# When the second image's attention values are emitted, and one pacing constant

## Chip, cores, metric

The kernel runs on one core of a Trainium2 chip. The metric is the device time of one execution in microseconds (us). The core has TensorE (PE; its weight loads are shown as PEld), VectorE (DVE), ScalarE (ACT) and GpSimd (POOL), each with a queue of its own that it executes in order, and SyncE (SP), whose queue issues the transfers (DMA).

## What is computed

The input x is four images of 128 channels and 64 x 64 pixels in float32. Four residual layers follow one another, and each reads the group norm of x (32 groups of four channels, no affine part):

```
x = x + attention(gn(x))      # one head over all 4096 pixels, 128 channels
x = x + conv5x5(gn(x))        # 5 x 5 weights built from two tables and their indices
x = x + scan(gn(x))           # state-space scan, 64 channels forward, 64 backward, 64 states each
x = x + conv3x3(gn(x))        # only main_w and main_b reach the output
```

The scan layer multiplies by Wx, applies a causal convolution of four taps and a silu, makes delta (a softplus), B and C by matrix products, and then runs, for each channel and each of 64 states, h[l] = exp(delta[l] A) h[l-1] + delta[l] x[l] B[l] and y[l] = sum over states of h[l] C[l], plus D x[l]; a last product by Wp gives the layer's output.

## The kernel before

Channels lie on the 128 partitions and the 4096 pixels along the free axis. Each image goes through a *front*: attention, the 5 x 5 convolution, and the *operands* of the scan (delta, delta times x, B and C, written to DRAM in four chunks of 1024 pixels). Then comes its scan, and after that its *back*: the product by Wp and the 3 x 3 convolution.

**Two streams in one program.** The order of instructions is written out by hand, with no reordering by the scheduler, and two Python generators are woven together. `scan_core` emits the scan. `work = images()` emits everything else: the fronts of the images 0 to 3, then the backs. The first image's front runs before any scan; from then on the scan of image b lies beside the front of image b+1, and the backs of images 0 to 2 lie beside the last scan.

**Ticks.** The scan of one image is 256 ticks (4 chunks x 2 directions x 16 groups of states x 2 groups of channels), 1024 for all. In a tick POOL makes the drive `db` (L1588), ACT the decay `da` (L1581, an exponential), DVE runs the recurrence over 1024 pixels (L1598), and the result is multiplied by C. The multiplication is done by DVE (L1601; I call that an *own* tick) or by POOL (L1619; a *pooled* tick). ACT copies the last state (L1614) so that the next chunk can go on from it. Every four ticks PE sums the states into `y` (L1637). Drives run two ticks ahead, the loads of the rows four ticks ahead.

**Narrow and wide form.** PSUM has four banks with the tags s, a, z, y, and four more that are used in one of two ways. In the *narrow* form they hold three half decays of 512 pixels and one bank for the operands, and each tick's decay, recurrence and own multiplication is done in two halves. In the *wide* form they hold two decays of 1024 pixels. `widen` (called once per tick) swaps the form after the recurrence of the tick in which the mark "narrow" is found set or gone.

**Marks.** The generators talk through a set `ready`. `scan_operands(b)` (from L1308 on) is a list of numbered slots, 5 per 512 pixels. It sets "operands" at its beginning, `(b, "taps")` at slot 39, when the last of PE's causal convolutions is out, and "drives" at slot 48. Slots 40 and 50 (first image) or 30 and 50 (the others) hook the logarithms of the softplus, which are emitted in the middle of the next tick (ACT has to load another function table for them and the first one again after them); the generator waits for that with yields of 0.4. After slot 50 it waits for two ticks to begin, emits the last join and drive, takes "operands", "drives" and "narrow" away, and sets `(b, "all")`. With "narrow" gone, the form becomes wide until the next image's convolution has ended and sets it again.

`to_pool(i)` decides which ticks are pooled, by i and by the marks at the time: i % 3 == 2 in the wide form; in the narrow form i % 5 in (0, 2, 4) while "operands" is set, only i % 5 == 1 once "drives" is set, and i % 5 in (1, 3) with neither.

**The values.** `attention_start(b, xn)` of the next image waits until the image before has set `(b - 1, "taps")`, takes the tile V (which held that image's normalised pixels), lets POOL set the column of ones (L483), and emits eight groups of four products of 128 x 128 x 128 on PE (`keys`, L496), each yielding SLOT = 0.7, and each group's copy from PSUM to V on ACT (`take`, L501). A group's bank is s or z in turn, but always s while "operands" is set. `both(...)` runs the operands of image b and the start of image b+1 in turn, one yield of each. When both are at their end, attention begins: a product and ACT's L532, then rounds of scores on PE (L746), exponentials on ACT (L759) and value products on PE (L767), 1.76 per round.

**The pace.** Each yield of `work` carries a cost in planned microseconds of PE. Per tick of scan b the loop hands out PACES[b] of cost, half of it in each half tick:

```
credit = min(credit + pace / 2, pace)
while credit > 0:
    credit -= next(work, pace)
```

Before an image's first tick, `before(b)` runs `work` without scan until `(b, "operands", 0)` is set, if it isn't yet.

Of the kernel before, what the change touches and what calls it, by code (L numbers as in the profile page):

```python
# [44 lines left out]

PRODUCT, VALUES, HOP, SLOT, AHEAD, EARLY = 0.86, 0.9, 1.7, 0.7, 4, 8
LAST_SHARE = 0.75
PACES = 2.60, 2.53, 2.53, 1.53


BQ, BK, BX, BP, CONVB, BD, DSKIP, MAINB, CONVW, ALOG = 0, 1, 2, 3, 4, 5, 6, 7, 8, 12
# [3 lines left out]
def conv_preact_kernel(  # L55
# [37 lines left out]
    pools, ready = {}, set()  # L93
    more = again = None

    def bank(tag, name):
        return pools.get(tag, ps).tile([P, MM], F32, tag=tag, name=name)
# [232 lines left out]
    def stats_tile(name):  # L330
        return small.tile([P, NM, 6], F32, tag=f"gn_st{name[0]}", name=f"st_{name}")
# [75 lines left out]
    def group_norm(st, name):  # L407


        def tile(tag, *shape):  # L410
            return small.tile([P, *shape], F32, tag=f"gn_{tag}", name=f"{tag}_{name}")

        nc.vector.bn_aggr(gcols[:, :, 0], st.rearrange("p a b -> p (a b)"))
        turned, after = gn_work[:, 0], gn_work[:, 1]
        nc.vector.transpose(turned, gcols.rearrange("p a b -> p (a b)"))
        means, vars_ = (
            turned[:, r * 32 : (r + 1) * 32].rearrange("p (g s) -> p g s", s=gsz) for r in range(2)
        )
        var, mean = (
            after[:, r * 32 : (r + 1) * 32].rearrange("p (g s) -> p g s", s=gsz) for r in range(2)  # L420
        )
        total = gn_sums[:, 0]
        nc.vector.tensor_reduce(total, means, AX.X, ALU.add)
        wide = total.unsqueeze(2).to_broadcast([P, 32 // gsz, gsz])
        nc.vector.tensor_scalar(mean, wide, -1.0 / gsz, None, ALU.mult)

        nc.vector.tensor_tensor(means, means, mean, ALU.add)
        nc.vector.tensor_tensor(means, means, means, ALU.mult)
        nc.vector.tensor_tensor(means, means, vars_, ALU.add)
        total = gn_sums[:, 1]  # L430
        nc.vector.tensor_reduce(total, means, AX.X, ALU.add)
        wide = total.unsqueeze(2).to_broadcast([P, 32 // gsz, gsz])
        nc.vector.tensor_scalar(var, wide, 1.0 / gsz, GN_EPS, ALU.mult, ALU.add)
        back = tile("back", 2, 32)
        nc.vector.transpose(back.rearrange("p a b -> p (a b)"), after)
        rs, nb = tile("rs", 1), tile("nb", 1)
        nc.gpsimd.tensor_tensor(rs, back[:, 0, 0:1], mhalf, ALU.pow)
        nc.gpsimd.tensor_tensor(nb, back[:, 1, 0:1], rs, ALU.mult)
        yield HOP
        return rs, nb  # L440

    def normalise(dst, src, gn):
        nc.scalar.activation(dst, src, AF.Identity, scale=gn[0], bias=gn[1])  # L443
# [27 lines left out]
    def attention_start(b, xn):  # L471

        if b == 0:
            st = stats_tile(f"a{b}")
            for i in range(NM):
                nc.vector.bn_stats(st[:, i, :], xn[:, bass.ts(i, MM)])
                yield 0.0
            gn = yield from group_norm(st, f"a{b}")
        while b > 0 and (b - 1, "taps") not in ready:
            yield 0.0  # L480
        v = pools["big"].tile([P, VSIZE], F32, tag="V", name=f"v_{b}")
        v = v[:, : NJT * (C + 1)].rearrange("p (j c) -> p j c", c=C + 1)
        nc.gpsimd.memset(v[:, :, C : C + 1], 1.0)  # L483
        pvs = {}

        def piece(i):
            cut = bass.ts(i, L // 4)
            if b == 0:
                normalise(xn[:, cut], xn[:, cut], gn)

        def keys(i):

            tag = "saz"[i % 3] if b == 0 else "s" if i % 2 == 0 or "operands" in ready else "z"
            pvs[i] = bank(tag, f"pv_{b}_{i}").rearrange("p (t c) -> p t c", c=C)
            for t in range(TPM):
                nc.tensor.matmul(  # L496
                    pvs[i][:, t, :], xn[:, bass.ts(i * TPM + t, P)], wv, start=True, stop=True
                )

        def take(i):  # L500
            nc.scalar.copy(v[:, i * TPM : (i + 1) * TPM, :C], pvs.pop(i))  # L501

        piece(0)
        yield SLOT
        for i in range(NM):
            if i % 2 == 0 and i // 2 + 1 < 4:
                piece(i // 2 + 1)
            keys(i)
            yield SLOT
            if b > 0:  # L510
                take(i)
                yield 0.0
            elif i > 0:
                take(i - 1)
        if b == 0:
            take(NM - 1)
        return xn, v
# [1220 lines left out]
    def program(safe):  # L1738
# [14 lines left out]
        def start(b, after=0):  # L1753

            while b > 0 and (b - 1, "read") not in ready:
                yield 0.0
            for _ in range(after):
                yield 0.0
            xn = large(b, f"x_{b}")[:, :L]
            yield from load(xn, normed[b] if b > 0 else xf[b])  # L1760
            for _ in range(after):
                yield 0.0
            return (yield from attention_start(b, xn))
# [101 lines left out]
        with ExitStack() as es, tc.manual_schedule():  # L1865
# [52 lines left out]
            pools["hc"] = es.enter_context(tc.tile_pool(name=f"hc{safe}", bufs=8))  # L1918
            pace = PACES[0]

            def before(b):
# [3 lines left out]
                while (b, "operands", 0) not in ready:  # L1925
                    next(work)
                pace = PACES[min(b, len(PACES) - 1)]

# [90 lines left out]
```

## Time and profile before

| | us |
|---|---|
| median of 3 runs | 4163.61 (4162.76 to 4168.47) |
| the profiled execution | 4165.07 |
| its span, first to last instruction | 4163.3 |
| mean granted TensorE clock | 0.938 of full speed |

| engine | busy us | share of the span |
|---|---|---|
| PE | 3664.0 | 88% |
| PEld | 2132.6 | 51% |
| DVE | 3509.3 | 84% |
| ACT | 2340.3 | 56% |
| POOL | 3537.9 | 85% |

Milestones in the span, read from the timeline: the first image's operands begin on PE at 625, the first drive of the scan starts at 663.5, the second image's values lie on PE from 679.0 to 712.3 and its scores from 717.4 to 1283. The second image's operands begin on PE at 1468.6, the third's at 2331.7, the fourth's at 3191.3. The last scan instruction ends near 4100, and the last image's back ends the span.

How to read it: a row of the profile's timeline gives the start of an instruction in us from the span's beginning, its length, its engine, its line in the kernel, its operation, the names of the tiles that it writes and reads, and, in square brackets, how long its engine stood idle before it and what ended that. A row of the view by stretches gives, for each engine, the busy time in the stretch and the number of instructions, then the clock that TensorE was granted, the share of time that the DMA engines were busy and what they moved in GB/s. Matmuls in float32 show as two instructions each.

### The profile page before, as it was taken

The page shows a single profiled execution, that of the slowest core. Times are in us where ns is not written, and L with a number is a line of the kernel's source. Part 1 is how long each engine was busy: PE and PEld are TensorE (multiplying, and loading weights), DVE is VectorE, ACT ScalarE, POOL GpSimd, SP SyncE. Part 2 cuts the span into 40 slices and gives each one's busy share as a digit, 9 for nine tenths or more (in the row PEclk, how much of TensorE's full clock was granted, in tenths as well). Part 3 has the DMA queues.
Part 4 walks back from the last instruction along what each step waited for, and adds up shares of the span by engine and source line. Part 5 has one row for each costly group of instructions (what it writes and reads, how often), then busy time and mean ns, then how long its engine had stood idle before and what let it go on. Part 6 is the DMA issues. An engine that isn't in the chain of part 4 may idle for free. (4 is left out here: it accounts for less than half of the span.)

```text
span 4163.3 us, 49791 instructions
## 1 busy us (share of the span) xinstructions
PE 3664.0 (88%) x17626; PEld 2132.6 (51%) x17626; DVE 3509.3 (84%) x2446; ACT 2340.3 (56%) x3925; POOL 3537.9 (85%) x1691
## 2 busy tenths in 40 slices
PE   8999997999999979999999889999899576676746
PEld 4444443888885337777763367777733121221212
DVE  3832216999999989999999889999998899999996
ACT  3344306667675476776654767766645654545442
POOL 3533315999999989999999899999999999999995
PEclk9999998999999989999999999999999788887967
DMA  1021006656555576555555665555656766666661
GB/s 66 30 76 66 3 10 232 211 189 195 191 191 193 194 248 223 199 186 197 191 188 187 232 231 195 193 192 188 203 178 205 273 199 235 206 202 234 208 239 57
DMA packets 224162, 742.39 MB, mean 178 GB/s; under 512 B 29710, under 2 KB 30990, under 8 KB 223644
## 3 DMA queue, kind: packets, MB, share of 16 engines
q1 hardware_dynamic: 223324, 738.73, 52.6%
q8 instruction: 140, 2.29, 0.2%
q14 instruction: 122, 1.00, 0.1%
q10 hardware_dynamic: 576, 0.37, 0.0%
HBM read 663.12 MB, written 75.87 MB: 178 GB/s over the span
## 5 line engine op out<-in xcount | busy, mean ns | idle before, releaser
L1588 POOL TENSOR_TENSOR db<-dx,br 128x1024 f32<-128x1024 f32 x1024 | 2400.0, 2371 | 105.0 <-DVE hc L1598 35.1
L1581 ACT ACTIVATE da<-de,a_neg 128x1024 f32<-128x1024 f32 (+1 forms) x1089 | 1162.1, 1068 | 363.9 <-DVE hc L1601 246.2
L1598 DVE TENSOR_TENSOR_SCAN da<-da,last,db 128x1024 f32<-128x1024 f32 (+1 forms) x501 | 1148.3, 2292 | 24.8 <-ACT da L1581 11.7
L1601 DVE TENSOR_TENSOR hc<-da,cr 128x1024 f32<-128x1024 f32 (+1 forms) x702 | 825.8, 1176 | 60.6 <-DVE da L1598 0.5
L1619 POOL TENSOR_TENSOR hc<-hc,cr 128x1024 f32<-128x1024 f32 x354 | 838.9, 2370 | 19.9 <-ACT last L1614 17.3
L746 PE MATMUL sc<-r,x 128*128 128x256 f32 x3072 | 808.3, 388 | 33.6 <-ACT exchange L759 25.7
L767 PEld LDWEIGHTS acc<-v,exchange 128*128 128x128 f32 x6144 | 801.1, 192 | 47.5 <-issue 10.9
L767 PE MATMUL acc<-v,exchange 128*128 128x129 f32 x6144 | 804.8, 275 | 0.4 <-ACT exchange L759 0.4
L1637 PE MATMUL y<-hc,sel 128*32 128x512 f32 x4096 | 596.8, 649 | 226.8 <-POOL hc L1619 171.6
L746 PEld LDWEIGHTS sc<-r,x 128*128 128x128 f32 x3072 | 530.8, 192 | 203.7 <-ACT last L1614 42.7
L1598 DVE TENSOR_TENSOR_SCAN hc<-da,last,db 128x1024 f32<-128x1024 f32 (+1 forms) x267 | 597.4, 2237 | 12.9 <-ACT last L1614 7.4
L759 ACT ACTIVATE exchange<-sc 128x512 f32<-128x512 f32 x768 | 444.6, 589 | 208.0 <-PE sc L746 195.3
L1637 PEld LDWEIGHTS y<-hc,sel 128*32 128x32 f32 x4096 | 114.1, 113 | 567.9 <-POOL hc L1619 240.2
L1598 DVE TENSOR_TENSOR_SCAN da<-da,db 128x1024 f32<-128x1024 f32 (+1 forms) x169 | 377.3, 2233 | 32.1 <-ACT da L1581 28.3
L568 POOL TENSOR_TENSOR sidep<-sidep,exchange 128x512 f32<-128x512 f32 x120 | 171.1, 1426 | 244.6 <-ACT exchange L550 242.1
L1614 ACT COPY last<-da 128x1 f32<-128x1 f32 x510 | 80.3, 157 | 504.8 <-DVE hc L1601 503.5
L550 ACT ACTIVATE exchange<-sc 128x512 f32<-128x512 f32 x256 | 152.8, 597 | 250.2 <-PE sc L549 246.7
L568 DVE TENSOR_TENSOR sided<-sided,exchange 128x512 f32<-128x512 f32 x120 | 98.1, 817 | 217.5 <-ACT exchange L550 216.2
L556 PE MATMUL acc<-exchange,v 128*128 128x512 f32 x512 | 263.3, 597 | 0.0
L549 PE MATMUL sc<-r,x 128*128 128x512 f32 x512 | 261.9, 594 | 0.8 <-ACT r L532 0.8
L922 PE MATMUL pcm<-xpm,cs 128*128 128x512 f32 x432 | 207.3, 628 | 7.5 <-ACT xpm L443 7.5
L1598 DVE TENSOR_TENSOR_SCAN hc<-da,db 128x1024 f32<-128x1024 f32 (+1 forms) x87 | 190.9, 2194 | 6.6 <-ACT last L1614 3.8
(296 smaller groups left out, 3028.8 us busy)
## 6 DMA issues: line engine op xcount, KB each, us to landing
br<-bm SPq DMA_DIRECT2D x512, 512.0 KB, 4.0
cr<-cm SPq DMA_DIRECT2D x512, 512.0 KB, 4.5
dx<-dxd SPq DMA_DIRECT2D x64, 512.0 KB, 5.3
de<-dd SPq DMA_DIRECT2D x64, 512.0 KB, 6.0
xs<-in_x_dram SPq DMA_DIRECT2D x16, 512.0 KB, 5.6
xsd<-xs SPq DMA_DIRECT2D x16, 512.0 KB, 3.8
bm<-bs SPq DMA_DIRECT2D x32, 256.0 KB, 4.6
xcd<-xc SPq DMA_DIRECT2D x16, 512.0 KB, 3.1
```

Source lines behind the costliest of these rows:

```text
L549: nc.tensor.matmul(sc, xn[:, bass.ts(j, P)], rq[blk], start=True, stop=True)
L556: nc.tensor.matmul(acc[blk], v[:, j, :C], ring[:, u % NRING, :], start=j == 0, stop=j == NJT - 1)
L568: eng.tensor_tensor(s, s, ring[:, u % NRING, :], ALU.add)
L746: nc.tensor.matmul(sc[:, bass.ts(n, HM)], xn[:, bass.ts(2 * k + n, P)], rq[blk][:, cut], start=n == 0, stop=True, skip_group_check=True,)
L759: nc.scalar.activation(pt, sc, AF.Exp)
L767: nc.tensor.matmul(acc[part][:, bass.ts(t, CV)], ring[:, u % NRING, n * HM + t * P : n * HM + (t + 1) * P], v[:, 2 * k + n, :], start=(k, ...
L1581: nc.scalar.activation(da, rep["de", b, c, d, g][:, bass.ts(h, size)], AF.Exp, scale=a_neg[:, at(i)])
L1588: nc.gpsimd.tensor_tensor(dbs[i], rep["dx", b, c, d, g], rows["b", b, c, d, q], ALU.mult)
L1598: nc.vector.tensor_tensor_scan(h, da, db[:, cut], before, ALU.mult, ALU.add)
L1601: nc.vector.tensor_tensor(hc[:, cut], h, rows["c", b, c, d, q][:, cut], ALU.mult)
L1619: nc.gpsimd.tensor_tensor(hcs[i], hcs[i], rows["c", b, c, d, q], ALU.mult)
L1637: nc.tensor.matmul(y[r : r + SG, :], sel, hcs[first + gg][:, bass.ts(h, MM)], start=False, stop=q == NQ - 1, tile_position=(0, r), skip_gr ...
```

## The change

The wait of `attention_start` is for another mark when b is 1, so for the values of the second image alone, and the first constant of PACES is 2.62 instead of 2.60. Nothing else differs; the third and fourth image's values still wait for "taps".

```
-PACES = 2.60, 2.53, 2.53, 1.53
+PACES = 2.62, 2.53, 2.53, 1.53
...
-        while b > 0 and (b - 1, "taps") not in ready:
+        while b > 0 and (b - 1, "all" if b == 1 else "taps") not in ready:
             yield 0.0
```

## The prediction

> **What bounds the kernel now.** I read the page first: the share of busy time of each engine and its 40 slices. The scans fill the span from 650 us on, and there DVE, POOL and, while attention or a convolution lies beside them, PE are all near full. Then I asked for the stretches of the first scan, which is where the change is:
>
> ```profile
> core 0: us, PE busy (x) PEld busy (x) DVE busy (x) ACT busy (x) POOL busy (x), PEclk, DMA share, GB/s
> 665.00:725.00 60.00, 36.54 (x142) 19.69 (x138) 45.21 (x50) 41.53 (x74) 49.94 (x26) 0.85 0.62 226
> 725.00:780.00 55.00, 54.84 (x366) 44.03 (x366) 48.05 (x28) 34.06 (x60) 48.99 (x22) 0.94 0.67 225
> 780.00:1280.00 500.00, 495.18 (x3436) 405.18 (x3429) 486.01 (x279) 352.32 (x638) 490.53 (x212) 1.00 0.59 193
> ```
>
> In 60 us with the operands beside the scan no engine is full; in the 500 us after it three are, within 3%. Ticks show the same: counted by DVE's scans, tick 0 starts at 673.3 and tick 10 at 724.7 (5.13 us each), tick 10 to 20 take 3.67 each, tick 20 to 184 take 3.160. The slow ticks are bound by a chain over in-order queues. DVE, the engine that has to do each tick's scan, waits here (timeline of DVE, columns start, length, operation, idle before it and what ended it):
>
> ```profile
> 690.28 0.70 DVE L1384 SCALAR_TENSOR_TENSOR pb<-u,pb 128x512 f32<-128x512 f32 x1 [4.70 <-ACT u L1413]
> ...
> 715.45 1.23 DVE L1598 TENSOR_TENSOR_SCAN da<-da,db 128x512 f32<-128x512 f32 x1 [2.22 <-ACT da L1581]
> ...
> 719.30 1.22 DVE L1598 TENSOR_TENSOR_SCAN da<-da,db 128x512 f32<-128x512 f32 x1
> ...
> 724.68 2.30 DVE L1598 TENSOR_TENSOR_SCAN da<-da,db 128x1024 f32<-128x1024 f32 x1 [1.43 <-ACT da L1581]
> ...
> 735.87 2.30 DVE L1598 TENSOR_TENSOR_SCAN da<-da,db 128x1024 f32<-128x1024 f32 x1 [4.61 <-ACT da L1581]
> ```
>
> The view of DVE's waits between 675 and 740 sums them: 8.3 for decays, 7.2 for the first image's steps, 0.7, together 16.2 us. Two of them (4.70 and 2.22) follow ACT's logarithms; 1.43 is the swap of the PSUM form; 4.61 is ACT, which stands with an exponential of attention while the next decay is behind it. PE's queue holds the values in between (timeline of PE):
>
> ```profile
> 686.48 2.07 PE L496 MATMUL pv<-wv,x 128*128 128x128 f32 x8 [6.40 <-ACT v L501]
> 688.35 2.86 PE L1364 MATMUL pb<-xc,bdiag 128*128 128x512 f32 x4
> 691.40 1.16 PE L496 MATMUL pv<-wv,x 128*128 128x128 f32 x8 [0.19 <-ACT v L501]
> 696.15 1.13 PE L1364 MATMUL pb<-xc,bdiag 128*128 128x512 f32 x2 [3.59 <-DVE bs L1370]
> ```
>
> With one bank for them (tag s while the operands run) the second group of values stands 6.40 us before a copy on ACT, and the products that the operands need are behind it.
>
> **What the change moves in the plan.** I added up the yields of both generators by hand, half tick by half tick (half the pace each, waits of 0.4 ended by the tick's events). For the old numbers this gives the swap to the wide form after tick 9, as the first 1024-wide scan at 724.68 (tick 10) shows. With the change: up to tick 0.5 nothing differs. Then the operands no longer share their half ticks: the last logarithms are hooked at tick 4 instead of 6, "all" comes at tick 6.0 instead of 8.0, the swap follows tick 7 instead of 9, and the eight groups of values lie in ticks 6.0 to 8.0 instead of 1 to 6.5, now over two banks. Attention begins at tick 8 in both. By 2.62 instead of 2.60 the later stages come one tick earlier: attention ends at 186 instead of 187, the second image's operands begin at 238 instead of 239, and so the third's (493 for 494) and the fourth's (748 for 749). Each narrow stretch there is as long as before. No drain is needed at an image's end: the first chunk of the next is made at tick 248.5 now, 252 is when it is needed.
>
> **The price of each part.**
>
> *Form and pooled ticks, first scan.* From DVE's rows, start to start: an own narrow tick 3.85 (715.45 to 719.30), a pooled narrow one 2.52 (706.84 to 709.36), an own wide one 3.53 (735.87 to 739.40), a pooled wide one 2.20 (742.93 to 745.13). Ticks 4 to 10 are now two pooled and four own narrow and one own wide: 5.04 + 15.40 + 3.53 = 23.97. After: tick 4 turns own (the "drives" mark comes at 3.5), 8 turns pooled, 8 and 9 wide: 11.55 + 2.52 + 2.20 + 7.06 = 23.33. **-0.6 us.** POOL's count of multiplies there is the same.
>
> *DVE's waits, first scan.* Of 16.2 us I keep the two after the logarithms (4.7 + 2.2), the swap 1.4 and the 0.7; the 2.5 for the last piece's u goes, because the product before it no longer stands behind values; for the 4.6 I put 3, since ACT then has eight copies of 0.59 (4.7 us) between the decays of ticks 7 to 9, though PE comes to attention without a gap. 16.2 - 12.0 = **-4.2 us**. Ends: only the logarithms' waits left, -9.3; all kept and the copies added, +4.7.
>
> *The later image ends.* The pooled choice goes by the tick's number, so a shift by one changes it: 258, 513, 762 and 766 are pooled now and own after. Own costs DVE 1.33 more (3.85 - 2.52) and POOL 2.37 less (row L1619 of the page). At 258, 513 and 766, the ticks of a swap, DVE waits 2.40 and 2.15 us for decays (at 1564.62 and 1568.06, the first of the three), which hides it; 762 has no such cover: **+1.3**. Ends: all four, +5.3; POOL was the one waited for at 762, -2.4.
>
> *The pace.* 0.02 more per tick is 158 x 0.02 = 3.2 us in the 500 us where PE is busy 495.2; it still fits, but only just. It shows where PE is full, the 55 us after 725: 17 ticks, **+0.4**. Ends: 0, and 0.02 x 229 ticks of attention and convolution, +4.6. Two other scans speak for the low end: at 2.53 their ticks take 3.157 and 3.163, at 2.60 3.160.
>
> *At nothing:* the memset of v (0.15 on POOL), now behind six more of POOL's steps, nobody before the copies waits for it. The sends of dd and dxd of the last chunk come two ticks earlier in SP's queue; now they hold SP from 708.5 to 720.5 and the row loads behind them, which run four ticks ahead; if that cover were gone, it shows as POOL's 1.5 us wait at 731.34. The new wait for "all" is in the plan alone, no instruction waits for it.
>
> Sum: -0.6 - 4.2 + 1.3 + 0.4 = **-3.1 us**. The profiled execution took 4165.07 (span 4163.3 and 1.8 around it), which gives 4162.0; it was 1.5 above the median of the three timed runs, 4163.61, and it is the median that I forecast: **4160.5 us**.
>
> A rule that speaks against the change. The granted clock in the trace is 0.77 from 680 to 695 and 0.80 from 695 to 710 while values and products share PE, and 0.69 from 725 to 735, when attention starts:
>
> ```profile
> 680.00:695.00 15.00, 5.96 (x21) 0.77 0.33 131
> 695.00:710.00 15.00, 9.69 (x44) 0.80 0.82 277
> 710.00:717.40 7.40, 3.48 (x22) 0.95 0.27 105
> 717.40:725.00 7.60, 4.54 (x12) 0.74 0.35 134
> 725.00:735.00 10.00, 9.84 (x50) 0.69 1.00 350
> ```
>
> The Trainium skill, "TensorE: Matmul & The Clock Gate", Part 1, says that the array runs at half clock by default and at full clock only after a window of about 3.4 us in which it was busy. By that rule, taking the values out leaves PE emptier in ticks 1 to 5, and five products at half clock would each last some 0.9 us more (an estimate from that page), 4.3 us on the operands' chain, with a sum of +1.2 instead of -3.1; the same rule gives some back at attention's start, which then follows the values directly. No row here shows PE without the values, so the sum is left as it is.
>
> **Rivals.**
> *The first scan loses all but the logarithms' waits.* For: the operands' chain is then alone on PE, and copies find two banks. Against: ACT's copies crowd the wide ticks. -0.6 - 9.3 + 0 + 0.4 = -9.5: **4154.1**.
> *POOL holds the first scan, the change does nothing there.* For: from 684.5 to 729.9 POOL has one gap of 0.9; its 44.4 us of steps stay the same ones. Against: by 731 it waits for DVE itself. -0.6 + 0 + 1.3 + 0.4 = +1.1: **4164.7**.
> *TensorE becomes the bound (slower).* The eight groups of values take about 1.05 each (row 679.02), 8.4 us. Now they lie where PE has 23 us idle of 60; then they lie directly before a stretch where it is 54.84 of 55 busy and 99.0% after. If PE never catches up, their 8.4 and the pace's 4.6 show: -0.6 + 8.4 + 4.6 = +12.4, **4176.0**. It decides when exponentials that wait for PE hold up decays by more than DVE's slack in the 500 us (14 us). Against: ticks at 2.53 are no shorter.
>
> **Chances.** Forecast 0.40, first scan frees up 0.22, POOL holds 0.25, TensorE binds 0.13. A measurement of this kernel tells about 0.2% (8.3 us) from no change. Faster by more: the first rival and a little of the forecast, 0.24; slower: the last, 0.13; within: 0.63. The range takes the first two rivals whole and part of the last, with the bounds of the later image ends: 4152 to 4172.
>
> **What would show it.** Swap: the first 1024-wide scan is tick 8, not 10, and two ticks earlier by the clock than 724.68 less what else went. Waits: DVE's sum from tick 1 to 13 near 12 us, no wait of PE for v among products. Image ends: tick 239 to 259 within 2 us of today's 101.4. Pace: ticks 20 to 184 at 3.16; 3.18 or more would be TensorE's rival. The forecast is wrong if DVE's waits at ticks 7 to 10 for decays exceed 8 us, or if an image's end differs by over 4 us, which I have no row for beyond the four moved multiplies.

## The result, and the profile after

The changed kernel takes 4173.27 us (median of 14 runs, 4167.7 to 4178.32), the kernel before 4164.47 beside it (14 runs, 4162.76 to 4168.47): ratio 1.0020, 95% interval 1.0013 to 1.0027. It is **slower by about 8.8 us**, outside the predicted range. The profiled execution of the changed kernel took 4170.89, its span is 4169.1, 5.8 more than before's 4163.3; its runs scatter more (10.6 us against 5.7), so the span shows only part of the median's loss.

Counted by DVE's scans, the time between ticks went as follows (us; the last column is pace_259r of the fourth set):

| ticks | what lies there | before | after | difference | best (old mark, 2.59) |
|---|---|---|---|---|---|
| 0 to 20 | operands, values, start of attention | 88.0 | 85.5 | -2.6 | 84.0 |
| 20 to 184 | attention of the second image | 518.2 | 521.9 | +3.6 | 517.3 |
| 184 to 236 | its convolution | 174.7 | 175.8 | +1.0 | 176.0 |
| 236 to 264 | second image's operands | 131.1 | 127.7 | -3.4 | 129.4 |
| 264 to 490 | attention and convolution, third image | 726.7 | 728.8 | +2.1 | 724.8 |
| 490 to 520 | its operands | 139.5 | 135.6 | -3.9 | 138.1 |
| 520 to 744 | attention and convolution, fourth image | 717.7 | 723.6 | +5.9 | 718.8 |
| 744 to 774 | its operands | 136.2 | 141.6 | +5.4 | 130.6 |
| 774 to 1023 | last scan, backs | 792.5 | 792.2 | -0.3 | 792.1 |

The first scan's stretches, changed kernel (same columns as in the prediction):

```profile
665.00:725.00 60.00, 36.80 (x131) 18.97 (x130) 44.85 (x46) 40.46 (x70) 49.26 (x26) 0.72 0.74 269
725.00:780.00 55.00, 55.00 (x384) 44.00 (x383) 51.02 (x30) 36.05 (x64) 51.87 (x23) 1.00 0.53 182
780.00:1280.00 500.00, 496.27 (x3446) 407.10 (x3445) 483.71 (x277) 352.37 (x639) 488.07 (x211) 1.00 0.58 192
```

PE is now busy in all of the 55 us from 725 (54.84 before) and has 3.7 us left of 500 (4.8 before). DVE and POOL do less in the same 500 us: 483.7 against 486.0, and 488.1 against 490.5. The timeline of DVE, rows with the longest waits:

```profile
687.82 0.69 DVE L1384 SCALAR_TENSOR_TENSOR pb<-u,pb 128x512 f32<-128x512 f32 x1 [3.62 <-ACT u L1413]
...
713.36 2.29 DVE L1598 TENSOR_TENSOR_SCAN hc<-da,db 128x1024 f32<-128x1024 f32 x1 [2.65 <-ACT da L1581]
...
719.65 2.30 DVE L1598 TENSOR_TENSOR_SCAN da<-da,db 128x1024 f32<-128x1024 f32 x1 [4.00 <-ACT da L1581]
...
723.65 2.30 DVE L1598 TENSOR_TENSOR_SCAN da<-da,db 128x1024 f32<-128x1024 f32 x1 [0.39 <-ACT da L1581]
```

The first 1024-wide scan is tick 8, as forecast. The waits of 4.61 and 2.22 are gone; two others, 2.65 and 4.00, stand where ACT now copies the values. The timelines of ACT and, below it, POOL show what these copies wait for:

```profile
704.95 1.32 ACT L1581 ACTIVATE da<-de,a_neg 128x512 f32<-128x512 f32 x2
710.89 1.07 ACT L501 COPY v<-pv 128x512 f32<-128x512 f32 x2 [4.62 <-POOL v L483]
711.85 0.20 ACT L1614 COPY last<-hc 128x1 f32<-128x1 f32 x1
711.95 0.17 ACT L1614 COPY last<-da 128x1 f32<-128x1 f32 x1
712.15 1.12 ACT L1581 ACTIVATE da<-de,a_neg 128x1024 f32<-128x1024 f32 x1
...
718.42 1.12 ACT L1581 ACTIVATE da<-de,a_neg 128x1024 f32<-128x1024 f32 x1
```

```profile
705.86 2.48 POOL L1392 TENSOR_TENSOR exchange<-exchange,u 128x512 f32<-128x512 f32 x2
708.42 2.35 POOL L1397 TENSOR_TENSOR xc<-exchange,xc 128x1024 f32<-128x1024 f32 x1
710.71 0.15 POOL L483 MEMSET v<- 128x32 f32 x1
```

The memset of v stands behind the last joins and the last drive of the operands; ACT's first copy waits 4.62 us for it, and the decay of tick 8 (712.15) is behind that copy. On PE no product of the operands stands behind a value that waits for its bank any more, but the values wait for the copies (7.49):

```profile
684.50 3.78 PE L1364 MATMUL pb<-xc,bdiag 128*128 128x512 f32 x4 [7.29 <-ACT last L1614]
689.89 2.08 PE L1364 MATMUL pb<-xc,bdiag 128*128 128x512 f32 x2 [1.60 <-DVE bs L1370]
...
711.53 8.21 PE L496 MATMUL pv<-wv,x 128*128 128x128 f32 x48 [7.49 <-ACT v L501]
```

A product of 128x512 shows as two instructions. It takes 2.08 us now (689.89) and took 1.13 before, and the stretches show the granted clock beside it:

```profile
680.00:695.00 15.00, 7.93 (x8) 2.18 (x8) 10.87 (x13) 12.98 (x23) 13.62 (x9) 0.50 0.39 158
695.00:710.00 15.00, 6.95 (x32) 3.39 (x32) 13.87 (x15) 8.03 (x13) 14.92 (x8) 0.61 0.74 250
710.00:717.40 7.40, 5.87 (x29) 5.87 (x30) 2.98 (x2) 3.87 (x8) 7.40 (x5) 0.54 0.88 313
717.40:725.00 7.60, 5.96 (x34) 4.51 (x33) 4.87 (x3) 5.69 (x10) 5.07 (x4) 1.00 0.97 348
725.00:735.00 10.00, 10.00 (x73) 7.82 (x72) 8.38 (x6) 6.39 (x12) 8.40 (x4) 1.00 0.46 155
```

The granted clock fell from 0.77 to 0.50 and from 0.80 to 0.61 where the values were taken out, and rose from 0.69 to 1.00 where attention starts.

**The fourth image's end.** SP's timeline, before and then after:

```profile
3268.09 0.51 SPq L1533 DMA_DIRECT2D dx<-dxd  x1
3268.65 1.23 SPq L1561 DMA_DIRECT2D xcr<-xcd  x2
3277.14 0.80 SPq L1393 DMA_DIRECT2D dd<-exchange  x2
3279.62 2.62 SPq L1398 DMA_DIRECT2D dxd<-xc  x2
...
3283.64 0.55 SPq L1533 DMA_DIRECT2D de<-dd  x1
```

```profile
3274.82 0.80 SPq L1393 DMA_DIRECT2D dd<-exchange  x2
3277.31 2.66 SPq L1398 DMA_DIRECT2D dxd<-xc  x2
...
3282.54 0.60 SPq L1533 DMA_DIRECT2D dx<-dxd  x1
...
3285.16 0.55 SPq L1533 DMA_DIRECT2D de<-dd  x1
```

Before, the last sends of dd and dxd are emitted in the first half of tick 765, behind the loads that go out in the second half of tick 764. One tick earlier they are ahead of these loads. SP issues in order here and the sends wait for the join, so the load of dx for tick 769 is issued at 3282.5 instead of 3268.1. POOL's drive for that tick waits for it (POOL after):

```profile
3291.92 4.63 POOL L1588 TENSOR_TENSOR db<-dx,br 128x1024 f32<-128x1024 f32 x2 [7.69 <-DMA dx<-dxd]
```

But it isn't this drive that ends DVE's wait. The drive ends at 3294.3, and DVE's scan of tick 769 starts at 3296.4, when ACT is done with a decay that waited for de, the load of the same tick's delta (DVE and ACT, before and then after):

```profile
3290.61 2.30 DVE L1598 TENSOR_TENSOR_SCAN da<-da,db 128x1024 f32<-128x1024 f32 x1 [2.77 <-ACT last L1614]
3289.39 1.12 ACT L1581 ACTIVATE da<-de,a_neg 128x1024 f32<-128x1024 f32 x1 [7.51 <-DMA de<-dd]
```

```profile
3296.41 2.30 DVE L1598 TENSOR_TENSOR_SCAN da<-da,db 128x1024 f32<-128x1024 f32 x1 [5.24 <-ACT last L1614]
3295.19 1.12 ACT L1581 ACTIVATE da<-de,a_neg 128x1024 f32<-128x1024 f32 x1 [10.33 <-DMA de<-dd]
```

In both kernels de is issued behind the sends. Before, two other transfers lie between the sends and de, and ACT has it 5.8 us after its issue; after, eight do, dx among them, and it takes 10.0 us. So the order of the sends delays DVE by all the loads behind them, not by dx alone. From the scan of tick 768 to that of 769 it is 10.5 us instead of 6.4: 4.1 of the stretch's +5.4 lie in this one tick.

At the second and third image the last sends go out 11.6 us or more behind the load of the same dx in both kernels; the fourth image's operands have no partner in `both` and end earlier, just beside those loads, and there a shift by one tick turns the order round.

### The profile page after: what moved, and what is told of

It is laid out like the page before. It is cut to its first block, busy times and chain, and to the rows that moved or that the text cites. A ratio compares the mean times of both kernels' runs of the same rounds, so it can differ in the third digit from the quotient of the medians.

```text
span 4169.1 us, 49780 instructions
## 1 busy us (share of the span) xinstructions
PE 3672.2 (88%) x17626; PEld 2132.7 (51%) x17626; DVE 3516.4 (84%) x2448; ACT 2337.1 (56%) x3923; POOL 3526.8 (85%) x1687
## 5 line engine op out<-in xcount | busy, mean ns | idle before, releaser
L1619 POOL TENSOR_TENSOR hc<-hc,cr 128x1024 f32<-128x1024 f32 x350 | 827.8, 2365 | 23.8 <-ACT last L1614 21.1
L1637 PE MATMUL y<-hc,sel 128*32 128x512 f32 x4096 | 608.3, 655 | 239.5 <-POOL hc L1619 171.5
```

The source lines that it names most:

```text
L1619: nc.gpsimd.tensor_tensor(hcs[i], hcs[i], rows["c", b, c, d, q], ALU.mult)
L1637: nc.tensor.matmul(y[r : r + SG, :], sel, hcs[first + gg][:, bass.ts(h, MM)], start=False, stop=q == NQ - 1, tile_position=(0, r), skip_gr ...
```

## The experiments

The theories. **Q**: the order of sends and loads in SP's queue at the fourth image's end. **M**: the multiplies that the shift moved from POOL to DVE. **T**: TensorE is the bound in the first scan's attention, so both a higher pace and values laid directly before it cost scan time. **A**: the shift by one tick itself, by where the operands' steps then fall. **P**: the memset behind POOL's steps. **G**: the mark itself gains. Ratios are against the kernel before on the same chip, with their intervals. In all kernels a pinned tick is forced own or pooled, the rest is left to `to_pool`.

### First set: the parts of the change, and the sends alone

gate_261, the new mark, with `PACES = 2.61, ...`; in the plan the later stages stand as in before. 

> The values wait for "all", as in the change, but the first pace is 2.61, which by the plan's sums brings the later narrow stretches back to the ticks they had before (239, 494, 749) while the first swap stays at tick 7. Theory Q (the loss is SP's queue at the fourth image's end, where the sends of delta now stand ahead of the load of dx): the order there is the old one, so the loss is gone and the first scan's 2 to 3 us stay: 4160 to 4163, ratio 0.9990 to 0.9997. Theory M (the loss is the four multiplies moved from POOL to DVE by the shift of one tick): the same, 4160 to 4163. Theory T (TensorE is the bound in the first scan, and the pace costs its own size): half of the 0.02 stays, +1.8 and the gate's values +4 to 8, 4168 to 4173.

pace_only, the old mark, with `PACES = 2.62, ...`. 

> 2.62 with the old mark "taps", so all of the shift by one tick and none of the gate. Theory Q: the SP order at the fourth image's end is the changed one, and the first scan's gain is missing: slower than before by 6 to 11 us, 4170 to 4175. Theory M: four multiplies, +1.3 to +5.3, 4166 to 4170. Theory T: 0.02 on 178 to 229 ticks, +3.6 to +4.6, about 4168.

after_hold, the change with

```
-                yield from next_tick()
-                yield from next_tick()
+                for _ in range(3 if b + 1 == B else 2):
+                    yield from next_tick()
```

and tick 766 pinned own. 

> The change, with the fourth image's last joins, sends and drives held for one more tick, and tick 766 kept an own one, so that only the place of these steps differs: SP again issues the load of dx for tick 769 ahead of the sends. Theory Q: POOL's wait for dx of 7.7 us goes, DVE's 5.2 and 1.8 us waits after tick 768 too, 4 to 6 us faster than the change: 4167 to 4169. Theories M and T: the same multiplies and the same pace, so as the change, 4172 to 4174, or 0.3 above it for one more narrow tick.

before_early, the kernel before with `range(1 if b + 1 == B else 2)` there, and tick 766 pinned pooled. 

> The kernel before, with the fourth image's last joins, sends and drives one tick earlier, and tick 766 kept a pooled one: the SP order of the change and nothing else of it. Theory Q: 4 to 6 us slower than before, 4168 to 4171, with POOL waiting for dx by 5 us or more near tick 769. Theories M and T: as before, 4163 to 4166.

| | median | ratio | ticks 20 to 170 | 744 to 774 |
|---|---|---|---|---|
| before | 4165.14 | | 474.7 | 136.2 |
| gate_261 | 4163.92 | 0.9998 (0.9989 to 1.0007) | 476.5 | 136.3 |
| pace_only | 4166.82 | 1.0006 (0.9997 to 1.0015) | 476.8 | 140.8 |
| after_hold | 4169.85 | 1.0012 (1.0003 to 1.0021) | 478.3 | 140.4 |
| before_early | 4170.10 | 1.0012 (1.0003 to 1.0021) | 475.0 | 139.6 |

before_early makes the kernel before 5 us slower; POOL's row there:

```profile
3286.64 2.34 POOL L1588 TENSOR_TENSOR db<-dx,br 128x1024 f32<-128x1024 f32 x1 [6.97 <-DMA dx<-dxd]
```

Tick 768 takes 12.1 us there against 6.4 before; the swap to the wide form comes a tick earlier too, and ticks 744 to 768 take 2.5 us less. So Q is a cause by itself. after_hold took POOL's wait away, and tick 768 takes 6.3 again, but the stretch's length stayed (140.4): holding back the operands' end also kept the narrow form a tick longer, and ticks 744 to 768 take 3.1 us more than in the change. So it didn't settle how much of the change's loss is Q. pace_only has the changed order as well (POOL waits 7.1 us for dx) and is still not clear of the kernel before, so Q alone isn't the whole loss. The pace alone, and the mark with the later stages left at their ticks (gate_261), cost little; the change costs more than both together.

### Second set: the pace, the mark, the multiplies

gate_260, the new mark with 2.60. 

> The changed mark alone, with the first pace left at 2.60. In the plan the swap to the wide form follows tick 7 as in the change, but what comes later moves the other way: the second image's operands come at 240 (before 239, changed kernel 238), the fourth image's last sends at tick 766.0 (before 765.0, changed kernel 764.0), so behind the loads that go out in the second half of tick 764. Theory Q (sends of dd and dxd ahead of the next loads in SP's queue) expects ticks 744 to 774 like before, 136.2 to 137, and no wait of POOL for dx. Theory T (TensorE is the bound in the first scan, and 0.02 more per tick is 0.02 us more) expects ticks 20 to 184 at 518.2 to 519, since the pace is the old one. Theory A (no bound: where the ends of attention's groups fall among own and pooled ticks decides, any shift moves it) expects 20 to 184 up to 3 us above 518.2. Ticks 0 to 20 at 85.2 by all (before 88.0). Total by Q and T: 3 us under before, ratio 0.9993; by Q and A: ratio 1.000.

gate_270, the new mark with 2.70. 

> The changed mark with a first pace of 2.70 instead of 2.62, five times the change's step, so that attention of the second image ends at tick 181 and its operands lie at 231 to 248. For the price of the pace; read ticks 20 to 170, 473.8 us in before (3.159 per tick) and 477.4 in the changed kernel. Theory T: TensorE is the bound there, so a tick's time goes with the pace, 0.10 x 150 = 15 us more than before, about 489. Theory A (phase, not the amount): within 4 us of before, 470 to 478. POOL as the bound, with TensorE's exponentials under it: 474. The end of the first image's operands moves by eight ticks, so its stretch and the total are not compared one by one; total by T about 12 us more than before, by A within 5.

after_pools, the change with ticks 258, 513, 762, 766 pinned pooled. 

> The changed kernel whole, with the four multiplies that the shift by one tick had moved from POOL to DVE (ticks 258, 513, 762, 766) given back to POOL. Theory M (the image ends' gain of 3.4 and 3.9 us, and part of the fourth image's loss, are these four multiplies: POOL was waited for) expects ticks 236 to 264 at 131.1 and 490 to 520 at 139.5 as in before, so 7 us lost, ratio 1.0035 against before. The rival, that the shift itself of the operands brings the gain, expects 127.7 and 135.6 as in the changed kernel and a ratio of 1.002. Theory Q expects ticks 744 to 774 at 140 or more in either, since the order in SP's queue stays the changed one.

before_own, the kernel before with ticks 258, 513 pinned own. 

> The kernel before with only the two multiplies of ticks 258 and 513 moved from POOL to DVE. Theory M expects the gains of the changed kernel at those two places, 236 to 264 at 127.7 (before 131.1) and 490 to 520 at 135.6 (before 139.5), the rest as before: 7 us faster, ratio 0.998. The rival (the shift of the operands is the gain) expects 131 and 139.5, and a ratio of 1.000. The price put on them in the prediction, nothing because DVE's waits for decays hide them, expects the same as this rival. If the stretches of attention after it give it back, 264 to 436 goes from 543.6 to 546 as in the changed kernel.

| | median | ratio | 20 to 170 | 236 to 264 | 490 to 520 | 744 to 774 |
|---|---|---|---|---|---|---|
| gate_260 | 4158.35 | 0.9986 (0.9977 to 0.9995) | 476.6 | 128.2 | 136.9 | 131.9 |
| gate_270 | 4178.82 | 1.0034 (1.0021 to 1.0048) | 485.2 | 119.0 | 127.0 | 124.9 |
| after_pools | 4171.15 | 1.0018 (1.0009 to 1.0027) | 478.5 | 127.6 | 135.7 | 144.3 |
| before_own | 4164.81 | 1.0001 (0.9992 to 1.0010) | 475.3 | 132.6 | 139.6 | 136.3 |

M falls: with the multiplies given back the gains at 236 and 490 stay, and moved alone they bring none. T holds in part: 0.10 of pace was to cost 15 us over 150 ticks and cost 10.5 against before (474.7; the 473.8 of the expectation was its mean per tick) and 8.6 against gate_260. The stretch from 780 to 1230, gate_270 and then before:

```profile
780.00:1230.00 450.00, 447.69 (x3110) 369.01 (x3103) 427.98 (x245) 315.69 (x577) 431.27 (x186) 1.00 0.58 189
```

```profile
780.00:1230.00 450.00, 445.18 (x3087) 363.88 (x3080) 437.05 (x251) 317.67 (x575) 440.96 (x191) 1.00 0.59 194
```

PE goes from 445.2 to 447.7 of 450, and DVE and POOL lose 9 and 10 us of work: more work per tick for a full PE buys fewer ticks. And gate_260 was a surprise: 6.8 us faster, with shorter image ends, although its shift is the opposite of the change's.

### Third set: mark or shift

pace_259, the old mark with 2.59; later stages as in gate_260. 

> The kernel before with 2.59 as the first pace and the old mark. In the plan everything after the first scan's tick 10 is then as in the kernel with the new mark and 2.60 (gate_260: operands at 240, 495 and 750), only the values of the second image still lie beside the first image's operands. It tells whether gate_260's 6.8 us are the new mark's or the shift's. Theory A (the shift by one tick is the gain, by where the operands' steps then fall): ticks 236 to 264 at 128.2, 490 to 520 at 137, 744 to 774 at 132 as there, total 4158 to 4160, ratio 0.9985 to 0.999. Theory G (the mark itself is the gain): ratio 0.9995 to 1.000, and the image ends as in before (131.1, 139.5, 136.2).

gate_258, the new mark with 2.58. 

> The new mark with 2.58 as the first pace: operands at 241, 496 and 751, one tick later still, and a lower price of the pace. Theory T (TensorE's share of the bound) expects ticks 20 to 170 at or a little below gate_260's 476.6. Theory A expects the image ends to move again, by up to 4 us each and without a direction that follows from the shift's sign (238: 127.7, 135.6, 141.6; 239: 131.1, 139.5, 136.2; 240: 128.2, 136.9, 131.9). A theory by which later operands are always better (Q alone) expects 744 to 774 at 132 or less and a ratio of 0.998.

before_phase, the kernel before with ticks 239 to 258, 494 to 513 and 749 to 766 pinned as gate_260 has them one tick later. 

> The kernel before with, in its three later narrow stretches (ticks 239 to 258, 494 to 513, 749 to 766), the choice of pooled and own ticks that gate_260 has one tick later, so that operands and pooled ticks stand to one another as they do there, while every slot of the operands stays at its tick. Six multiplies more on DVE in all. Theory A in its narrow form (the standing of the operands' steps against the pooled ticks is what the shift changes) expects 236 to 264 at 128.2 instead of 131.1, 490 to 520 at 136.9 instead of 139.5, 744 to 774 at 131.9 instead of 136.2, total 4156, ratio 0.9977. The rival (what counts is where the operands stand against the chunk's and image's first ticks, their loads and copies) expects no such gain: each within 1.5 us of before or slower, ratio 1.000 to 1.001.

hold_phase, after_hold with ticks 748 to 766 pinned as the kernel before has them one tick later. 

> The changed kernel with the fourth image's last joins and sends one tick later (as in after_hold) and, from tick 748 to 766, the choice of pooled and own ticks that the kernel before has one tick later. Theory A in its narrow form: 744 to 774 goes from after_hold's 140.4 to before's 136.2, total 4165.5, ratio 1.0002. The rival (the place against the image's first tick): stays at 139.5 to 141.5, ratio 1.0012. Theory Q: no wait of POOL for dx behind those sends in either.

| | median | ratio | 0 to 100 | 236 to 264 | 490 to 520 | 744 to 774 |
|---|---|---|---|---|---|---|
| before | 4164.50 | | 340.1 | 131.1 | 139.5 | 136.2 |
| pace_259 | 4151.39 | 0.9967 (0.9955 to 0.9979) | 334.1 | 129.9 | 137.8 | 132.6 |
| gate_258 | 4164.57 | 0.9999 (0.9990 to 1.0008) | 336.9 | 131.6 | 140.0 | 137.3 |
| before_phase | 4160.91 | 0.9990 (0.9981 to 0.9999) | 338.8 | 131.5 | 136.0 | 134.8 |
| hold_phase | 4169.77 | 1.0013 (1.0004 to 1.0022) | 342.0 | 127.6 | 135.8 | 142.0 |

The old mark with 2.59 is 13 us faster than the kernel before, the fastest of all kernels here. Its image ends are those of gate_260 within 2 us, so the shift is what shortens them (A), and G falls. The way goes no further: with 241 (gate_258) the ends are as long as before. The narrow form of A, that only the standing of the operands against own and pooled ticks counts, met its number at one place of four (136.0 at 490 to 520), a third of the gain at another (134.8, 1.4 of 4.3), and failed at 236 to 264 (131.5) and in hold_phase (142.0).

At the fourth image SP's queue shows most of what the shift does. With the operands at 240 the sends come late enough for de, too, to go out ahead of them (SP of gate_260):

```profile
3270.89 0.55 SPq L1533 DMA_DIRECT2D de<-dd  x1
3274.22 0.80 SPq L1393 DMA_DIRECT2D dd<-exchange  x2
```

DVE then has no wait at tick 769, and tick 768 takes 3.5 us in gate_260 and pace_259, against 6.4 before: 2.9 of the 4.3 and 3.6 us that are gained there. At the second and third image the gains are spread over many ticks, and no such place was found.

### Fourth set: the mark alone, the sends alone

gate_259, the new mark with 2.59. 

> The new mark with 2.59 as the first pace; in the plan it differs from pace_259 (4151.4) in the first scan's ticks 0 to 10 alone, so it shows the mark's own price. Theory T (the values, moved from beside the operands to directly before attention, delay attention's start by some 4 to 6 us on a TensorE that is then full): 4156 to 4159, ratio 0.998 to 0.9987, ticks 0 to 100 at 337 to 338 against pace_259's 334.1. The theory of the prediction (the mark frees 2.5 to 4 us of DVE's waits): 4148, ratio 0.996, ticks 0 to 100 at 331.

after_late, the change with

```
-                yield from next_tick()
-                yield from next_tick()
+                yield from next_tick(); yield from next_tick()
+                for _ in iter(lambda: b + 1 == B and "half" not in ready, False): yield late_hooks.append(lambda: ready.add("half")) or 0.4
```

> The changed kernel with the fourth image's last joins, drives and sends half a tick later, so that in SP's queue they come behind the loads of the same tick, as they do before the change; the swap stays at tick 765 and every tick is own or pooled as in the changed kernel. Theory Q (those sends hold back the load of dx for tick 769): no wait of POOL for dx, ticks 768 to 772 give 4 us back, 744 to 774 at 137.5 against 141.6, total 4169, ratio 1.0010 to 1.0012. The rival (the operands' place, one tick earlier, makes the fourth image's end long by itself): 744 to 774 stays at 140 or more, ratio 1.0015 to 1.002.

pace_258, the old mark with 2.58. 

> The kernel before with 2.58 as the first pace: operands at 241, 496 and 751. Theory T: ticks 20 to 170 at 473 to 474 (2.59: 473.7, 2.60: 474.7, 2.62: 476.8), as TensorE is not the bound below 2.60. The image ends as with the new mark and 2.58: 131.6, 140.0 and 137.3, so what 2.59 gained there is lost: total 4157 to 4160, ratio 0.9983 to 0.999. If a later start of the operands is a gain by itself, as the way from 2.62 over 2.60 to 2.59 would have it: 4150 or less.

pace_259r, pace_259 once more. 

> The kernel of pace_259 once more, beside the others of this batch on the same chip. If its gain stands: ratio 0.996 to 0.9975, ticks 0 to 20 at 82 to 83, image ends at 130, 137.8 and 132.6. If it was an accident of that batch: ratio 0.998 to 1.000.

| | median | ratio | 0 to 100 | 20 to 170 | 744 to 774 |
|---|---|---|---|---|---|
| before | 4163.85 | | 340.1 | 474.7 | 136.2 |
| gate_259 | 4156.25 | 0.9982 (0.9973 to 0.9992) | 339.1 | 475.7 | 131.7 |
| after_late | 4166.96 | 1.0006 (0.9997 to 1.0015) | 342.8 | 478.6 | 137.4 |
| pace_258 | 4168.93 | 1.0008 (0.9999 to 1.0018) | 339.1 | 474.8 | 136.5 |
| pace_259r | 4149.68 | 0.9962 (0.9948 to 0.9975) | 335.6 | 473.8 | 130.6 |

after_late settles Q: 141.6 became 137.4, as expected, and the ratio went from 1.0020 to 1.0006, further than forecast. Tick 768 takes 3.5 us instead of the change's 10.5, and ticks 744 to 768 take 2.9 more. SP issues dx at 3270.46 again, ahead of the sends, and POOL's drives run on without a wait (SP, then POOL of after_late):

```profile
3270.46 0.51 SPq L1533 DMA_DIRECT2D dx<-dxd  x1
3271.02 1.23 SPq L1561 DMA_DIRECT2D xcr<-xcd  x2
3275.66 0.80 SPq L1393 DMA_DIRECT2D dd<-exchange  x2
3278.13 2.63 SPq L1398 DMA_DIRECT2D dxd<-xc  x2
```

```profile
3280.39 9.24 POOL L1588 TENSOR_TENSOR db<-dx,br 128x1024 f32<-128x1024 f32 x4
```

gate_259 and pace_259r differ in the mark alone: at this pace it **costs 6.6 us**, 3.5 of them by tick 100. Two other pairs differ in the mark alone, at the same shift. At 2.62 (pace_only and the change, ratios 1.0006 and 1.0020) it costs 5.8 us, 3.9 by tick 100 (338.0 and 341.9). At 2.58 (pace_258 and gate_258, 1.0008 and 0.9999) it costs nothing (the two intervals overlap), and 2.2 us are gained by tick 100. The gain of 2.59 stands (0.9962). pace_258 loses it all, and was missed by 9 us: its ends are as long as before's, and ticks 0 to 100 too.

DVE's rows show why the mark doesn't gain here where the prediction saw it gain. pace_259r, with the old mark, and then gate_259:

```profile
715.98 1.23 DVE L1598 TENSOR_TENSOR_SCAN da<-da,db 128x512 f32<-128x512 f32 x1 [2.21 <-ACT da L1581]
...
725.21 2.30 DVE L1598 TENSOR_TENSOR_SCAN da<-da,db 128x1024 f32<-128x1024 f32 x1 [1.43 <-ACT da L1581]
...
730.94 2.27 DVE L1598 TENSOR_TENSOR_SCAN da<-da,db 128x1024 f32<-128x1024 f32 x1
```

```profile
715.39 2.29 DVE L1598 TENSOR_TENSOR_SCAN hc<-da,db 128x1024 f32<-128x1024 f32 x1 [2.59 <-ACT da L1581]
720.77 2.30 DVE L1598 TENSOR_TENSOR_SCAN da<-da,db 128x1024 f32<-128x1024 f32 x1 [3.10 <-ACT da L1581]
...
730.09 2.29 DVE L1598 TENSOR_TENSOR_SCAN hc<-da,db 128x1024 f32<-128x1024 f32 x1 [1.71 <-PE y L1637]
```

The wait of 4.61 at tick 12 is gone with the old mark too. It belonged to the exact pace, not to the place of the values alone: 2.62 and 2.59 with the old mark haven't it, 2.58 has 3.13 there. With it goes a gap of 3.19 us on PE, at 725 in the kernel before: the granted clock is 0.69 from 725 to 735, and the 16 instructions of attention's value products there take 3.65 us. 2.58 with the old mark has the gap too (3.20). pace_259r hasn't: the 16 instructions, at 723.3, take 1.95, and its clock from 725 to 735 is 1.00.

### Fifth set: what the mark costs

gate_259_ones is gate_259, and after_mended after_late, both with

```
-        while b > 0 and (b - 1, "all" if b == 1 else "taps") not in ready:
-            yield 0.0
+        while b > 0 and (b - 1, "taps") not in ready: yield 0.0
...
         nc.gpsimd.memset(v[:, :, C : C + 1], 1.0)
+        while b == 1 and (b - 1, "all") not in ready: yield 0.0
```

> gate_259 (new mark, 2.59) with the tile v taken and its memset issued at the old mark, so that it stands in POOL's queue before the last joins and drives; the values still begin at the new mark. Theory P (the memset behind POOL's steps is the price): ACT's wait of 4.57 for it at its first copy is gone, DVE's wait of 2.59 at tick 8 too, attention starts 3 to 5 us earlier against tick 0 (52.6 now), ticks 0 to 100 at 335 to 336, total 4151 to 4153, ratio 0.9968 to 0.9973. Theory T (8.4 us of values directly before a full TensorE are the price): ACT's wait goes, but ticks 0 to 100 stay at 338 to 339 and the total at 4155 to 4157, ratio 0.998.

> The changed kernel (new mark, 2.62) with both suspected causes of its loss taken away: the memset of v at the old mark, and the fourth image's last joins and sends half a tick later (as in after_late). Theories P and Q together: ticks 744 to 774 at 137.5, ticks 0 to 100 at 339 instead of 341.9, total 4162 to 4164, ratio 0.9995 to 1.000. Theory T with Q: ticks 0 to 100 at 341 to 343, total as after_late, 4167, ratio 1.0006.

gate_259_ones took 4159.35, ratio 0.9981 (0.9972 to 0.9990), after_mended 4166.30, ratio 0.9999 (0.9990 to 1.0008). ACT's wait for the memset is gone:

```profile
708.84 1.06 ACT L501 COPY v<-pv 128x512 f32<-128x512 f32 x2
...
717.36 0.59 ACT L501 COPY v<-pv 128x512 f32<-128x512 f32 x1 [1.68 <-PE pv L496]
719.07 0.59 ACT L501 COPY v<-pv 128x512 f32<-128x512 f32 x1 [1.12 <-PE pv L496]
719.55 1.12 ACT L1581 ACTIVATE da<-de,a_neg 128x1024 f32<-128x1024 f32 x1
```

But the later copies still wait for PE, the decay of tick 9 stands behind them as before (719.55 in both), DVE's waits at ticks 8 to 10 add up to 6.3 us against 6.1, and the time is the same: 0.9981 against 0.9982, ticks 0 to 100 at 338.0 against 339.1. At 2.59 P was visible and not the price.

At 2.62 it is not settled. after_mended gained 1.6 us by tick 100 against the change (340.2), 2.6 against after_late, and its ratio is the one that P and Q together forecast, not the 1.0006 of T with Q, though the intervals of after_mended and after_late overlap. It kept Q's gain (137.9); the change without both faults is no different from before.

What is left at 2.59 is T's account, by elimination: no run isolates it. Attention's first exponential starts 52.0 us after tick 0 here and 52.6 in gate_259, against 47.6 in pace_259r, so PE is some 5 us behind. It is as late at 2.58 (52.3 with the new mark, 46.7 with the old), where the mark costs nothing. That fits T, by which the delay is a price only where the pace leaves PE little room, but it doesn't prove it.

## Why the prediction was wrong, by its steps

- **The sends, "At nothing": the step that failed.** It followed the moved sends of dd and dxd in SP's queue at the first image alone, where they come two ticks earlier, and there it was right: POOL has no wait for a transfer in ticks 0 to 24. The pace moved the same sends at the other three images, and at the fourth it turned their order against the loads: POOL waited 7.69 us for dx, ACT 10.33 for de, and tick 768 took 10.5 us instead of 6.4. With the order put back (after_late) the stretch is 137.4 instead of 141.6, and the kernel takes 4166.96 us, inside the stated range and not clear of the kernel before. The prediction asked at the image ends only about four multiplies and whether the chunk was made in time.
- **The pace, +0.4, mis-sized.** (17 ticks of 0.02 are 0.3, to begin with.) It was paid in the whole attention of the second image, not in 55 us: over ticks 20 to 170, 476.8 against 474.7 with the old mark, 478.3 to 478.6 against 476.6 with the new. Ticks 20 to 184 took 3.182 each, which the prediction had named as the sign of TensorE's rival. Its evidence against that rival, the ticks at 2.53, says nothing about the price at higher paces: with the old mark 2.58, 2.59 and 2.60 give 474.8, 473.8 and 474.7, so there the price sets in above 2.60. With the new mark it rises from lower paces on (473.3, 475.7 and 476.6).
- **TensorE's rival** fits these stretches, with too high a price: it set 8.4 for the values and 4.6 for the pace, and 20 to 170 shows 1.9 for the new mark alone (gate_260) and 2.1 for the pace alone (pace_only).
- **DVE's waits, -4.2: right in the sum, not for its reason.** From tick 1 to 13 those over 0.5 us are 12.4, against 12.0 forecast. At 2.60 the mark alone would have done it (12.5 in gate_260). But the pace alone does so too (12.9 in pace_only), because the wait of 4.61 goes with any of several paces, so in the change the mark adds next to nothing; at 2.59 it raises the sum (13.7 in gate_259, 11.8 in pace_259r). That the sum came out at the forecast is in part luck.
- **The memset, "At nothing".** A copy did wait for it, 4.62 us, and the next decay behind the copy. gate_259_ones shows that at 2.59 it cost next to nothing in the total; at 2.62 after_mended leaves up to some 3 us open.
- **Form and pooled ticks, -0.6**, and the plan: tick 8 is the first wide one. Ticks 0 to 20 gained 2.6 of the 4.8 that this term and DVE's waits give, and the pace alone gains 2.4 there (85.6 in pace_only).
- **The later image ends, +1.3**: the first two were 3.4 and 3.9 shorter instead, by the shift, not by the multiplies (after_pools). The fourth's +5.4 passed the 4 us that the prediction set as its limit.
- **The rule that spoke against the change.** The Trainium skill, "TensorE: Matmul & The Clock Gate", Part 1, makes the clock depend on PE being busy. The trace agrees both ways, 0.77 to 0.50 beside the operands and 0.69 to 1.00 at attention's start. A product took 2.08 us instead of 1.13, 0.95 more, so the prediction's estimate from that page, 0.9, held. The 4.3 us on the operands' chain didn't show: DVE's waits for the first image's steps fell from 7.2 to 3.9 us, and leaving the rule out of the sum did no harm.

**What stays open.** Why the operands' stretch at the second and third image gets shorter or longer by 3 to 4 us with a shift of one tick: 236 to 264 is 127.7, 131.1, 128.2 and 131.6 with operands at 238, 239, 240 and 241. It was shown to be the shift, not the multiplies, and not the standing against pooled ticks alone. The 5.9 us lost from 520 to 744 were not traced either; part of them is scatter, as after_late, with the same plan there, has 721.3 against before's 717.7. And of the mark's 6.6 us at 2.59, 3.5 lie in the first 100 ticks; the rest isn't placed.

## What to carry to other kernels

When an edit shifts a plan by one step, follow every queue at **every** repetition of that step, above all a queue of transfers that issues in order, as SP's does here: a send that waits for compute, emitted half a tick earlier, can hold back a load that waits for nothing. Then ask which of the loads behind it is waited for last: here POOL's wait for dx was the first to be seen, and ACT's for de the one that held DVE. Work that is moved to lie directly before a stretch where an engine is full is not free because it was taken from a stretch where that engine was idle; here it delayed attention's start by some 5 us. And before a wait is credited to the thing that one means to move, run the kernel with a neighbouring value of its constants: here 2.59 instead of 2.60, with nothing moved, brought 13 us.

## What the runs showed of the hardware that was not expected

SP issued a load 12.9 us after POOL's drive had freed its buffer (3269.6, end of the drive that starts at 3267.25, to 3282.5), behind two pairs of sends that waited for their data and some loads; the loads' lead of four ticks was used up by it. A load of de of 512 KB was there 10.0 us after its issue when eight other transfers had been issued between it and the sends, 5.8 us when two had. The kernel's time moves by up to 0.46% with a shift of one tick, in which only a few multiplies change engines: 2.58, 2.59, 2.60 and 2.62 with the old mark take 1.0008, 0.9962, 1 and 1.0006 of the time before.
